# Two layers of cross-attention and expert MLP: last expert of layer 0 finished block by block, two contexts of layer 1 taken ahead, first block of the last stage taken without the block tables

## Chip, cores and metric

The kernel runs on one core of a Trainium2 chip, in one launch. The metric is the device time of that core in microseconds (us), as the median of the runs. All arithmetic shown here is in 32-bit floats. TensorE multiplies, VectorE (DVE), ScalarE (ACT) and GpSimd (POOL) do the rest, and SyncE (SP) issues most of the DMAs.

## What is computed

There are 16 sequences of 128 tokens with 512 features, and one context of 128 rows for each sequence. Four residual steps follow one another:

```python
x = x + L0_xattn(layernorm(x), ctx)      # two attentions, 16 heads
x = x + L0_ffn(layernorm(x))             # 8 experts, top 2, capacity 640
x = x + L1_xattn(layernorm(x), ctx)      # keys/values of context and tokens
x = x + L1_ffn(layernorm(x))             # 8 experts, top 2, no capacity
# L0 expert:  relu(x_e @ w1) @ w2, 512 -> 2048 -> 512, times the gate
# L1_xattn:   k, v from [ctx ; tokens]; q and k RMS-normed, then RoPE
# L1 expert:  (silu(x @ w1_gate) * (x @ w1_up)) @ w2, 512 -> 352 -> 512
```

The change leaves all of this as it is; it concerns the order of the work in the last three steps, and some buffers.

## The kernel before

The program has four stages, one after the other.

**Layer-0 attention** (class `Layer0`) is not touched.

**Layer-0 experts** (`Experts0`). Each of the 8 experts has 640 slots in five blocks of 128 rows. An expert's hidden width of 2048 is cut into 16 slices. `first(e, k)` multiplies the transposed rows of the expert by one slice of w1 in two halves of 320 columns, into the PSUM banks h0 and h1, and applies the relu into `hT` (h0 on ScalarE, h1 on VectorE). `second(e, k)` adds that slice's product with w2 to five PSUM banks o0 to o4, one for each block; each bank has one buffer. The loop in `run` issues `first` one slice ahead of `second`. In the 16th slice `result(e, b)` scales bank b by the gate weight into a tile `y` (even b on ScalarE, odd b on VectorE), and GpSimd adds y into the table in DRAM with an indirect DMA (a scatter). The scatters of one table are chained: each waits for the one before to have landed. The rings are `y` 5 buffers, `hT` 3, `w1` and `w2` 3 each. Gathers of the next expert's rows, the rope tables (`rope_tables`) and the loads of layer 1's weights are spread over the slices as well.

**Layer-1 attention** (`Layer1`). The steps of one sequence are named in the list `ORDER1`, each with a lag in periods; period p takes each step for sequence p minus its lag, so six and more sequences are in flight. Every engine keeps exactly this program order (the class `InOrder` records each instruction in order, which is why its line, L65, stands for nearly all instructions in the profile). For a sequence's context the steps are: `Kp0` (key projection, TensorE), `Ksq0` (squares, ScalarE), `Krs0` (inverse root on GpSimd), `Kn0` (normalise, VectorE), `Ka0` and `Kb0` (the two RoPE products, VectorE and GpSimd), `Ks0` (their sum), `Vp0` and `V0` (value projection and copy), `Ktr0` and `KT0` (transposes and copy). Its tokens go through `ldx` (load), `ln1`, `lnp`, `lnn` (layer norm), `trX` (transpose), `hT` (copy), and then `Vp1`, `Kp1`, `Qp0` and the rest. `load_first` loads the context `cT` and the rope table `rp`. All tiles of this stage lie in the pool `c_work`, which is opened after the experts' pool is closed and takes over its memory. The weights lie in the pool `c_w`, which is opened before the experts' pool.

**Layer-1 experts** (`Blocks1`). The chosen rows are cut into 39 blocks of 128, each of one expert; which, is known only on the chip. At the stage's start SP is given 16 loads of `e_w`, the weights of all 8 experts (1408 KB and 768 KB for each), and after them `rows_behind` (a tile `e_zero` of zeros, written to the spare rows of the output). `tables` then computes from the routing counts which expert and which slots each block has: some twenty small VectorE steps, and at the end two matmuls that pick the slots, and `slot_rows`, which makes of them the rows to gather (`e_source`) and to scatter to (`e_target`). Then a software pipeline runs over the blocks: gather (GpSimd) four periods ahead, transposes, `first` (h0 and h1), `gate` (silu on ScalarE), `product` (VectorE), transposes, `second`, and the scatter into the output. TensorE addresses a block's weights through a register that is loaded from the tables (`register`), and `first` reads from a view that covers the weights of all experts up to the block's largest possible one.

Of the kernel before, what the change touches and what calls it, by code (L numbers as in the profile page):

```python
# [22 lines left out]
P = 128  # L23
# [6 lines left out]
E = 8  # L30
# [842 lines left out]
    )  # L873


def slot_rows(ops, pool, tokens, n):


    nc, t = ops.nc, ops.t
    ids = t(pool, [P, n], F32, "e_ids")  # L880
    nc.vector.tensor_scalar(ids, tokens, -1.0, None, ALU.add)
    source = t(pool, [P, n], I32, "e_source")
    nc.vector.tensor_scalar(source, ids, 0.0, None, ALU.max)
    behind = t(pool, [P, 1], F32, "e_behind")
    nc.vector.tensor_scalar(behind, ops.tok[:, 0:1], float(SPAN + 1), None, ALU.add)
    empty = t(pool, [P, n], F32, "e_empty")
    nc.vector.tensor_scalar(empty, ids, 0.0, behind, ALU.is_lt, ALU.mult)
    target = t(pool, [P, n], I32, "e_target")
    nc.vector.tensor_tensor(target, ids, empty, ALU.add)
    return source, target  # L890

# [54 lines left out]
class Experts0:  # L946
# [4 lines left out]

    SLICES = FF0 // P

    def __init__(self, ops, tc, args, router, x_dram, sum_dram, work, psum):
        self.ops, self.args, self.work, self.psum = ops, args, work, psum
# [20 lines left out]
    def weights(self, e, f):  # L978
        nc, t = self.ops.nc, self.ops.t
        w1 = t(self.work, [P, NC, 256], F32, "w1", 3)  # L980
        nc.sync.dma_start(out=w1, in_=self.args["f0_w1"][e, f])
        w2 = t(self.work, [P, 2, D], F32, "w2", 3)
        nc.sync.dma_start(out=w2, in_=self.args["f0_w2"][e, f])
        self.w[e, f] = w1, w2

    def first(self, e, k):
        nc, t = self.ops.nc, self.ops.t
        if k % 2 == 0:
            self.weights(e, k // 2)
        w1, at = self.w[e, k // 2][0], k % 2 * P  # L990
        hT = self.h[e, k] = t(self.work, [P, CAP], F32, "hT", 3)
        half = CAP // 2
        for i in range(2):
            s = slice(i * half, i * half + half)
            ps = t(self.psum, [P, half], F32, f"h{i}")
            for c in range(NC):
                nc.tensor.matmul(
                    ps, w1[:, c, at : at + P], self.xT[e][:, c, s],
                    start=(c == 0), stop=(c == NC - 1),
                )  # L1000
            if i:
                nc.vector.tensor_scalar(hT[:, s], ps, 0.0, None, ALU.max)
            else:
                nc.scalar.activation(hT[:, s], ps, AF.Relu)

    def second(self, e, k):
        nc, t = self.ops.nc, self.ops.t
        if k == 0:
            self.outs[e] = [t(self.psum, [P, D], F32, f"o{b}") for b in range(NBLK0)]
        hT, w2 = self.h.pop((e, k)), self.w[e, k // 2][1]  # L1010
        for b in range(NBLK0):
            nc.tensor.matmul(
                self.outs[e][b], hT[:, b * P : (b + 1) * P], w2[:, k % 2, :],
                start=(k == 0), stop=(k == self.SLICES - 1),
            )
            if k == self.SLICES - 1:
                self.result(e, b)

    def result(self, e, b):

        nc = self.ops.nc
        y = self.ops.t(self.work, [P, D], F32, "y", 5)
        col = self.column(e, b)
        weight = self.table[:, P + col : P + col + 1]
        if b % 2:
            nc.vector.tensor_scalar(y, self.outs[e][b], weight, None, ALU.mult)
        else:
            nc.scalar.activation(y, self.outs[e][b], AF.Copy, scale=weight)
        scatter_add(self.ops, self.sum_dram, self.target[:, col : col + 1], y)

    def run(self, extra):
        for b in range(NBLK0):
            self.fetch(0, b)
            self.turn(0, b)
        steps = [(e, k) for e in range(E) for k in range(self.SLICES)]
        for i, (e, k) in enumerate(steps):
            self.first(e, k)
            if i:
                self.second(*steps[i - 1])
            if e + 1 < E and k % 2 == 0:  # L1040
                b = k // 2 - 2
                if 0 <= b + 2 < NBLK0:
                    self.fetch(e + 1, b + 2)
                if 0 <= b < NBLK0:
                    self.turn(e + 1, b)
            if i >= 4 and extra:
                extra.pop(0)()
        self.second(*steps[-1])


def layer0_experts(ops, tc, args, router, x_dram, sum_dram, extra):
# [33 lines left out]
class Layer1:  # L1085

    def __init__(self, ops, args, x_rows, w, rope_dram, router, out, work, banks):
        self.ops, self.args, self.x_rows, self.rope_dram = ops, args, x_rows, rope_dram  # L1090
        self.wq, self.wk, self.wv, self.wo = w
        self.router, self.out, self.work, self.banks = router, out, work, banks
        self.at = [{} for _ in range(NB)]

    def load_first(self, b):

        t, nc, s = self.ops.t, self.ops.nc, self.at[b]
        s["cT"] = t(self.work, [P, NC, P], F32, "cT", 2)
        nc.sync.dma_start(out=s["cT"], in_=self.args["ctxT"][b])
        s["rp"] = t(self.work, [P, 3, 2, P], F32, "rp", 3)  # L1100
        nc.sync.dma_start(out=s["rp"].rearrange("p i s h -> p (i s h)"), in_=self.rope_dram[b])

    def load_x(self, b, tag, bufs):
        s = self.at[b]
        s[tag] = self.ops.t(self.work, [P, D], F32, tag, bufs)
        self.ops.nc.sync.dma_start(out=s[tag], in_=self.x_rows[b])

    def step(self, name, b):
# [164 lines left out]
    def run(self):  # L1273
        lags = dict(ORDER1)
        last = max(lags.values())
        for period in range(NB + last):
            for b, call in (
                (period - lags["Kp0"] + 1, self.load_first),
                (period - lags["xr"] + 1, lambda b: self.load_x(b, "xr", 3)),
            ):  # L1280
                if 0 <= b < NB:
                    call(b)
            for name, lag in ORDER1:
                if 0 <= period - lag < NB:
                    self.step(name, period - lag)
            if period >= last:
                self.at[period - last].clear()


def layer1_attention(ops, tc, args, x_rows, w, rope_dram, router, out):  # L1290
    with ExitStack() as ctx:
        work = ctx.enter_context(tc.tile_pool(name="c_work", bufs=1))
        psum2 = ctx.enter_context(tc.tile_pool(name="c_ps", bufs=2, space=PSUM))
# [7 lines left out]
                return pool.tile(shape, dt, name=name, tag=tag)  # L1301

        scheduled, ops.nc = ops.nc, Engines(tc, ops.nc)
        Layer1(ops, args, x_rows, w, rope_dram, router, out, work, Banks()).run()
        ops.nc = scheduled


class Blocks1:
# [8 lines left out]
    def __init__(self, ops, tc, args, router, x_dram, out, small, work, psum):  # L1317
# [1 line left out]
        self.x_dram, self.out, self.work, self.psum = x_dram, out, work, psum  # L1319
        nc, t = ops.nc, ops.t  # L1320
        self.w = t(small, [P, E, FW], F32, "e_w")
        for e in range(E):
            rows = slice(e * P, (e + 1) * P)
            nc.sync.dma_start(out=self.w[:, e, :FW1], in_=args["f1_w1"][rows, :])
            nc.sync.dma_start(out=self.w[:, e, FW1:], in_=args["f1_w2"][rows, :])
        rows_behind(ops, small, out)
        self.tables(small)
        self.at = [{} for _ in range(NBLK1)]

    def tables(self, small):  # L1330

        ops, nc, t, router = self.ops, self.ops.nc, self.ops.t, self.router
        iota = ops.iota
        n = SPAN // P
        pc = t(self.psum, [P, D], F32, "po")
        nc.tensor.matmul(pc[:, :E], ops.ones, router.macc, start=True, stop=True)
        count = t(small, [P, E], F32, "count")
# [42 lines left out]
        nc.vector.scalar_tensor_tensor(place, eb, float(n), place, ALU.mult, ALU.add)  # L1380
        pick = t(small, [P, NBLK1], F32, "pick")
        nc.vector.tensor_scalar(pick, place, ops.tok[:, 0:1], None, ALU.is_equal)
        pi = t(self.psum, [P, D], F32, "po")
        for i in range(2):
            nc.tensor.matmul(
                pi[:, i * P : i * P + NBLK1], router.table[:, i * P : (i + 1) * P], pick,
                start=True, stop=True,
            )
        self.weight = t(small, [P, NBLK1], F32, "e_weight")
        nc.vector.tensor_copy(self.weight, pi[:, P : P + NBLK1])  # L1390
        self.source, self.target = slot_rows(ops, small, pi[:, :NBLK1], NBLK1)

    def gather(self, j, s):
        s["g"] = self.ops.t(self.work, [P, D], F32, "g", 4)
        gather(self.ops, s["g"], self.x_dram, self.source[:, j : j + 1])

    def register(self, j, s):
        last = min(j, E - 1)  # L1400
# [28 lines left out]
    def gate(self, j, s):  # L1429
        s["act"] = self.ops.t(self.work, [P, FF1], F32, "act", 2)  # L1430
        self.ops.nc.scalar.activation(s["act"], s["h", 0], AF.Silu)

    def product(self, j, s):
        self.ops.nc.vector.scalar_tensor_tensor(
            s["act"], s["act"], self.weight[:, j : j + 1], s["h", 1], ALU.mult, ALU.mult
        )

    def turn_act(self, j, s):
# [22 lines left out]
        self.ops.nc.scalar.copy(s["y"], s["po"])  # L1461

    def add(self, j, s):
        scatter_add(self.ops, self.out, self.target[:, j : j + 1], s["y"])

    def run(self):
        self.plain, self.ops.nc = self.ops.nc, Engines(self.tc, self.ops.nc)
# [22 lines left out]
def xattn_moe_two_layers(ctx: ExitStack, tc: tile.TileContext, args, out):  # L1490
# [26 lines left out]
    with tc.tile_pool(name="c_w", bufs=1) as wpool:  # L1517
# [5 lines left out]
        def ahead(work):  # L1523
# [10 lines left out]

        layer0_experts(ops, tc, args, router0, x0_dram, x_dram, ahead)
        layer1_attention(
            ops, tc, args, x_rows, (wq, wk, wv, wo), rope_dram, router1, out
        )
    layer1_experts(ops, tc, args, router1, x1_dram, out)

# [71 lines left out]
```

## Time and profile before

| what | value |
|---|---|
| median of 3 runs | 3967.91 us (3963.16 to 3968.94) |
| profiled execution | 3962.43 us, its span 3960.7 us |
| granted TensorE clock over the span | 0.974 of full |
| layer-0 attention | 0 to about 1390 us |
| layer-0 experts | about 1397 to 2536 us |
| layer-1 attention | about 2568 to 3612 us |
| layer-1 experts | about 3612 to 3960 us |

The profile is of one execution. Its columns of time are microseconds from the span's start. In the timeline, the bracket at the end of a row gives how long the engine was idle before it, and what released it. A matmul of 32-bit floats appears as two instructions, so that a projection with four matmuls of 128x512 is listed as x8. In the names, `o<-w,hT` is an operation that writes tile o and reads w and hT; `x_dram<-y` is a scatter of a y.

### The profile page before, as it was taken

The numbers are of one execution on the slowest core, as the hardware profiler recorded it, in microseconds if no ns is written. First come the engines' busy times: TensorE is split into PE (matmuls) and PEld (weight loads), VectorE is DVE, ScalarE is ACT, GpSimd is POOL, SyncE is SP. The second block draws the span as 40 slices with busy tenths as digits, with TensorE's granted clock in tenths as the row PEclk, the third lists the DMA queues.
The fourth block names the chain that finished last, engine by engine and source line by source line (L and its number), as shares of the span: only waits on it lengthen the run. The fifth ranks groups of instructions, "written<-read, shape, count | busy, mean of one in ns | idle before, by whom it ended". The sixth has DMA issues, their size and how long they took to land. (4 is left out here: it accounts for less than half of the span.)

```text
span 3960.7 us, 44119 instructions
## 1 busy us (share of the span) xinstructions
PE 3762.5 (95%) x14481; PEld 2417.1 (61%) x14481; DVE 1873.6 (47%) x4335; ACT 1369.1 (35%) x5089; POOL 1205.3 (30%) x1488
## 2 busy tenths in 40 slices
PE   5999899899999889999999999699999999997998
PEld 3776677688788755555555555355555555554565
DVE  7878877777788823100000000055555555553111
ACT  4665555566766401000000000043443433341111
POOL 7446655644522123111011000042222222220332
PEclk8999999899999989999999999899999999998999
DMA  5223332322322253233233232200000100005433
GB/s 170 90 94 117 115 105 95 120 91 96 115 81 81 72 191 99 93 90 82 61 91 85 65 85 72 57 22 25 28 31 22 31 22 29 18 11 207 75 65 56
DMA packets 134818, 312.45 MB, mean 79 GB/s; under 512 B 15872, under 2 KB 16000, under 8 KB 132800
## 3 DMA queue, kind: packets, MB, share of 16 engines
q1 hardware_dynamic: 116896, 268.21, 20.8%
q0 software_dynamic: 17696, 41.43, 5.7%
q8 instruction: 117, 1.92, 0.2%
q14 instruction: 109, 0.89, 0.1%
HBM read 231.72 MB, written 77.86 MB: 78 GB/s over the span
## 5 line engine op out<-in xcount | busy, mean ns | idle before, releaser
L65 PE MATMUL h<-xT,w 128*128 128x320 f32 x2048 | 574.8, 434 | 4.1 <-ACT hT L65 4.1
L65 PE MATMUL o<-w,hT 128*128 128x512 f32 x1280 | 570.0, 592 | 0.0
L65 PEld LDWEIGHTS h<-xT,w 128*128 128x128 f32 x2048 | 387.9, 191 | 191.1 <-issue 43.7
L65 DVE TENSOR_SCALAR hT<-h 128x320 f32<-128x320 f32 x128 | 62.9, 492 | 784.4 <-PE h L65 776.3
L65 PEld LDWEIGHTS o<-w,hT 128*128 128x128 f32 x1280 | 243.2, 190 | 265.5 <-issue 245.1
L65 ACT ACTIVATE hT<-h 128x320 f32<-128x320 f32 x128 | 55.8, 436 | 923.0 <-PE h L65 923.0
L65 POOL DMA_INDIRECT x_dram<-y,e_target x40 | 62.8, 1571 | 867.3 <-ACT y L65 717.4
L65 ACT ACTIVATE p<-sc,sm_nm 128x128 f32<-128x128 f32 (+1 forms) x768 | 300.9, 408 | 25.0 <-DVE sm_nm L65 14.4
L65 PE MATMUL mm<-w,xq 128*128 128x512 f32 x1024 | 294.6, 432 | 14.4 <-ACT raw L65 7.6
L65 PE MATMUL po<-w,cq 128*128 128x512 f32 x1024 | 274.2, 410 | 6.3 <-DVE cq L65 6.3
L65 PE MATMUL sc<-kT,qT 128*128 128x128 f32 (+1 forms) x1536 | 266.8, 310 | 5.9 <-ACT p L65 5.9
L65 PEld LDWEIGHTS sc<-kT,qT 128*128 128x128 f32 x1536 | 222.6, 191 | 63.2 <-issue 45.7
L65 PE MATMUL pv<-pT,v 128*128 128x256 f32 (+1 forms) x768 | 257.7, 459 | 1.4 <-ACT pT L65 1.4
L65 ACT ACTIVATE hn_sq<-mm 128x128 f32<-128x128 f32 x768 | 213.3, 278 | 121.1 <-PE mm L65 102.0
L65 DVE TENSOR_REDUCE sm_nm<-sc 128x4 f32<-128x512 f32 (+1 forms) x256 | 176.0, 687 | 140.6 <-PE sc L65 138.9
L65 PEld LDWEIGHTS mm<-w,xq 128*128 128x128 f32 x1024 | 198.8, 200 | 60.0 <-ACT raw L65 8.4
L65 PE MATMUL po<-c_wo,oT 128*128 128x512 f32 x512 | 231.4, 595 | 0.0
L65 PE MATMUL mm<-c_wq,hT 128*128 128x512 f32 x512 | 230.4, 593 | 0.4 <-DVE qn L65 0.4
L65 PEld LDWEIGHTS po<-w,cq 128*128 128x128 f32 x1024 | 185.7, 191 | 42.8 <-DVE cq L65 7.2
L65 POOL TENSOR_TENSOR hn_rs<-hn_rs,mhalf 128x4 f32<-128x4 f32 x192 | 197.2, 1027 | 16.0
L65 ACT ACTIVATE rms_sq<-mm 128x128 f32<-128x128 f32 x384 | 106.8, 278 | 273.2 <-PE mm L65 227.2
L65 PE MATMUL h<-e_w,xT 128*128 (+1 forms) x624 | 199.1, 462 | 1.7 <-DVE xT L65 1.7
(213 smaller groups left out, 6241.8 us busy)
## 6 DMA issues: line engine op xcount, KB each, us to landing
w<-in_f_w SPq DMA_DIRECT2D x128, 512.0 KB, 3.7
x_dram<-xr SPq DMA_DIRECT2D x64, 256.0 KB, 2.0
xr<-x_dram SPq DMA_DIRECT2D x64, 256.0 KB, 2.9
e_w<-in_f_w SPq DMA_DIRECT2D x8, 1408.0 KB, 22.3
xk<-in_ctxT SPq DMA_DIRECT2D x32, 256.0 KB, 2.8
xv<-in_ctxT SPq DMA_DIRECT2D x32, 256.0 KB, 3.3
raw<-in_wproj SPq DMA_DIRECT2D x32, 256.0 KB, 3.0
lnT<-kept_lnT SPq DMA_DIRECT2D x32, 256.0 KB, 3.2
```

What stands on the lines that cost most here:

```text
L65: return self.tc.keep_in_program_order(call(*args, **kwargs))
```

## The change

It has three parts.

- In `Experts0` the last `HELD` = 6 slices of the last expert are not taken slice by slice: their `first` steps run in a row, and then block after block takes all six second products, so that each block's result follows its own six. For this the rings of `hT` and `w2` grow to 7 and 5. The ring of `y` goes from 5 to 3, for all experts.
- In `Layer1` the tiles `cT`, `rp` and `xn` move to the pool `c_w`. The context steps of the first two sequences (`CONTEXT`) are issued ahead of the first period, one sequence after the other, and left out of the periods later.
- In `Blocks1` SP loads only the weights of expert 0 at the start, and `rows_behind` follows at once. The two loads of expert j+1 are issued on ScalarE's queue, behind the silu of block j, for j = 0 to 6. Block 0, which is always the first block of expert 0, gets its slots from the first column of the identity instead of the tables (`slots`), and its gather is issued before the tables are computed; the tables follow, and serve the other blocks (`column`).

```diff
@@ -873,19 +873,19 @@
-def slot_rows(ops, pool, tokens, n):
+def slot_rows(ops, pool, tokens, n, tag="e"):
...
@@ -951,7 +951,9 @@
     SLICES = FF0 // P
+    HELD = 6
     def __init__(self, ops, tc, args, router, x_dram, sum_dram, work, psum):
         self.ops, self.args, self.work, self.psum = ops, args, work, psum
@@ -979,7 +981,7 @@
         nc, t = self.ops.nc, self.ops.t
         w1 = t(self.work, [P, NC, 256], F32, "w1", 3)
         nc.sync.dma_start(out=w1, in_=self.args["f0_w1"][e, f])
-        w2 = t(self.work, [P, 2, D], F32, "w2", 3)
+        w2 = t(self.work, [P, 2, D], F32, "w2", self.HELD // 2 + 2)
         nc.sync.dma_start(out=w2, in_=self.args["f0_w2"][e, f])
         self.w[e, f] = w1, w2
@@ -988,7 +990,7 @@
         if k % 2 == 0:
             self.weights(e, k // 2)
         w1, at = self.w[e, k // 2][0], k % 2 * P
-        hT = self.h[e, k] = t(self.work, [P, CAP], F32, "hT", 3)
+        hT = self.h[e, k] = t(self.work, [P, CAP], F32, "hT", self.HELD + 1)
         half = CAP // 2
         for i in range(2):
             s = slice(i * half, i * half + half)
@@ -1003,12 +1005,12 @@
             else:
                 nc.scalar.activation(hT[:, s], ps, AF.Relu)
-    def second(self, e, k):
+    def second(self, e, k, blocks=range(NBLK0)):
         nc, t = self.ops.nc, self.ops.t
         if k == 0:
             self.outs[e] = [t(self.psum, [P, D], F32, f"o{b}") for b in range(NBLK0)]
-        hT, w2 = self.h.pop((e, k)), self.w[e, k // 2][1]
-        for b in range(NBLK0):
+        hT, w2 = self.h[e, k], self.w[e, k // 2][1]
+        for b in blocks:
             nc.tensor.matmul(
                 self.outs[e][b], hT[:, b * P : (b + 1) * P], w2[:, k % 2, :],
                 start=(k == 0), stop=(k == self.SLICES - 1),
@@ -1019,7 +1021,7 @@
     def result(self, e, b):
         nc = self.ops.nc
-        y = self.ops.t(self.work, [P, D], F32, "y", 5)
+        y = self.ops.t(self.work, [P, D], F32, "y", 3)
         col = self.column(e, b)
         weight = self.table[:, P + col : P + col + 1]
         if b % 2:
@@ -1033,9 +1035,10 @@
             self.fetch(0, b)
             self.turn(0, b)
         steps = [(e, k) for e in range(E) for k in range(self.SLICES)]
+        held = len(steps) - self.HELD
         for i, (e, k) in enumerate(steps):
             self.first(e, k)
-            if i:
+            if 0 < i <= held:
                 self.second(*steps[i - 1])
             if e + 1 < E and k % 2 == 0:
                 b = k // 2 - 2
@@ -1045,7 +1048,9 @@
                     self.turn(e + 1, b)
             if i >= 4 and extra:
                 extra.pop(0)()
-        self.second(*steps[-1])
+        for b in range(NBLK0):
+            for e, k in steps[held:]:
+                self.second(e, k, (b,))
 def layer0_experts(ops, tc, args, router, x_dram, sum_dram, extra):
@@ -1086,8 +1091,14 @@
-    def __init__(self, ops, args, x_rows, w, rope_dram, router, out, work, banks):
+    AHEAD = 2
+    CONTEXT = (
+        "Kp0", "Ksq0", "Krs0", "Kn0", "Ka0", "Kb0", "Ks0", "Vp0", "V0", "Ktr0", "KT0"
+    )
+    def __init__(self, ops, args, x_rows, w, rope_dram, router, out, first, work, banks):
         self.ops, self.args, self.x_rows, self.rope_dram = ops, args, x_rows, rope_dram
+        self.first_pool = first
         self.wq, self.wk, self.wv, self.wo = w
         self.router, self.out, self.work, self.banks = router, out, work, banks
         self.at = [{} for _ in range(NB)]
@@ -1095,14 +1106,15 @@
     def load_first(self, b):
         t, nc, s = self.ops.t, self.ops.nc, self.at[b]
-        s["cT"] = t(self.work, [P, NC, P], F32, "cT", 2)
+        s["cT"] = t(self.first_pool, [P, NC, P], F32, "cT", 2)
         nc.sync.dma_start(out=s["cT"], in_=self.args["ctxT"][b])
-        s["rp"] = t(self.work, [P, 3, 2, P], F32, "rp", 3)
+        s["rp"] = t(self.first_pool, [P, 3, 2, P], F32, "rp", 3)
         nc.sync.dma_start(out=s["rp"].rearrange("p i s h -> p (i s h)"), in_=self.rope_dram[b])
     def load_x(self, b, tag, bufs):
         s = self.at[b]
-        s[tag] = self.ops.t(self.work, [P, D], F32, tag, bufs)
+        pool = self.first_pool if tag == "xn" else self.work
+        s[tag] = self.ops.t(pool, [P, D], F32, tag, bufs)
         self.ops.nc.sync.dma_start(out=s[tag], in_=self.x_rows[b])
     def step(self, name, b):
@@ -1273,21 +1285,29 @@
     def run(self):
         lags = dict(ORDER1)
         last = max(lags.values())
+        self.done = set()
+        for b in range(self.AHEAD):
+            self.load_first(b)
+        for b in range(self.AHEAD):
+            for name in self.CONTEXT:
+                self.step(name, b)
+                self.done.add((name, b))
         for period in range(NB + last):
             for b, call in (
                 (period - lags["Kp0"] + 1, self.load_first),
                 (period - lags["xr"] + 1, lambda b: self.load_x(b, "xr", 3)),
             ):
-                if 0 <= b < NB:
+                if 0 <= b < NB and (call != self.load_first or b >= self.AHEAD):
                     call(b)
             for name, lag in ORDER1:
-                if 0 <= period - lag < NB:
+                if 0 <= period - lag < NB and (name, period - lag) not in self.done:
                     self.step(name, period - lag)
             if period >= last:
                 self.at[period - last].clear()
-def layer1_attention(ops, tc, args, x_rows, w, rope_dram, router, out):
+def layer1_attention(ops, tc, args, x_rows, w, rope_dram, router, out, first):
     with ExitStack() as ctx:
         work = ctx.enter_context(tc.tile_pool(name="c_work", bufs=1))
         psum2 = ctx.enter_context(tc.tile_pool(name="c_ps", bufs=2, space=PSUM))
@@ -1301,7 +1321,7 @@
-        Layer1(ops, args, x_rows, w, rope_dram, router, out, work, Banks()).run()
+        Layer1(ops, args, x_rows, w, rope_dram, router, out, first, work, Banks()).run()
...
@@ -1319,19 +1339,39 @@
         self.x_dram, self.out, self.work, self.psum = x_dram, out, work, psum
         nc, t = ops.nc, ops.t
         self.w = t(small, [P, E, FW], F32, "e_w")
-        for e in range(E):
-            rows = slice(e * P, (e + 1) * P)
-            nc.sync.dma_start(out=self.w[:, e, :FW1], in_=args["f1_w1"][rows, :])
-            nc.sync.dma_start(out=self.w[:, e, FW1:], in_=args["f1_w2"][rows, :])
+        self.load(nc.sync, 0)
         rows_behind(ops, small, out)
+        self.at = [{} for _ in range(NBLK1)]
+        self.blocks = None
         self.tables(small)
-        self.at = [{} for _ in range(NBLK1)]
+    def load(self, queue, e):
+        rows = slice(e * P, (e + 1) * P)
+        queue.dma_start(out=self.w[:, e, :FW1], in_=self.args["f1_w1"][rows, :])
+        queue.dma_start(out=self.w[:, e, FW1:], in_=self.args["f1_w2"][rows, :])
+    def slots(self, small, which, n, tag):
+        nc, table = self.ops.nc, self.router.table
+        ps = self.ops.t(self.psum, [P, D], F32, "po")
+        for i in range(2):
+            nc.tensor.matmul(
+                ps[:, i * P : i * P + n], table[:, i * P : (i + 1) * P], which,
+                start=True, stop=True,
+            )
+        source, target = slot_rows(self.ops, small, ps[:, :n], n, tag)
+        weight = self.ops.t(small, [P, n], F32, f"{tag}_weight")
+        nc.vector.tensor_copy(weight, ps[:, P : P + n])
+        return source, target, weight
     def tables(self, small):
         ops, nc, t, router = self.ops, self.ops.nc, self.ops.t, self.router
         iota = ops.iota
         n = SPAN // P
+        self.block0 = self.slots(small, ops.ident[:, 0:1], 1, "e0")
+        self.gather(0, self.at[0])
         pc = t(self.psum, [P, D], F32, "po")
         nc.tensor.matmul(pc[:, :E], ops.ones, router.macc, start=True, stop=True)
         count = t(small, [P, E], F32, "count")
@@ -1380,21 +1420,18 @@
         nc.vector.scalar_tensor_tensor(place, eb, float(n), place, ALU.mult, ALU.add)
         pick = t(small, [P, NBLK1], F32, "pick")
         nc.vector.tensor_scalar(pick, place, ops.tok[:, 0:1], None, ALU.is_equal)
-        pi = t(self.psum, [P, D], F32, "po")
-        for i in range(2):
-            nc.tensor.matmul(
-                pi[:, i * P : i * P + NBLK1], router.table[:, i * P : (i + 1) * P], pick,
-                start=True, stop=True,
-            )
-        self.weight = t(small, [P, NBLK1], F32, "e_weight")
-        nc.vector.tensor_copy(self.weight, pi[:, P : P + NBLK1])
-        self.source, self.target = slot_rows(ops, small, pi[:, :NBLK1], NBLK1)
+        self.blocks = self.slots(small, pick, NBLK1, "e")
+    def column(self, i, j):
+        return self.blocks[i][:, j : j + 1] if j else self.block0[i]
     def gather(self, j, s):
-        s["g"] = self.ops.t(self.work, [P, D], F32, "g", 4)
-        gather(self.ops, s["g"], self.x_dram, self.source[:, j : j + 1])
+        if "g" not in s:
+            s["g"] = self.ops.t(self.work, [P, D], F32, "g", 4)
+            gather(self.ops, s["g"], self.x_dram, self.column(0, j))
     def register(self, j, s):
         last = min(j, E - 1)
@@ -1429,10 +1466,12 @@
     def gate(self, j, s):
         s["act"] = self.ops.t(self.work, [P, FF1], F32, "act", 2)
         self.ops.nc.scalar.activation(s["act"], s["h", 0], AF.Silu)
+        if j + 1 < E:
+            self.load(self.ops.nc.scalar, j + 1)
     def product(self, j, s):
         self.ops.nc.vector.scalar_tensor_tensor(
-            s["act"], s["act"], self.weight[:, j : j + 1], s["h", 1], ALU.mult, ALU.mult
+            s["act"], s["act"], self.column(2, j), s["h", 1], ALU.mult, ALU.mult
         )
     def turn_act(self, j, s):
@@ -1461,7 +1500,7 @@
         self.ops.nc.scalar.copy(s["y"], s["po"])
     def add(self, j, s):
-        scatter_add(self.ops, self.out, self.target[:, j : j + 1], s["y"])
+        scatter_add(self.ops, self.out, self.column(1, j), s["y"])
     def run(self):
         self.plain, self.ops.nc = self.ops.nc, Engines(self.tc, self.ops.nc)
@@ -1534,7 +1573,7 @@
-            ops, tc, args, x_rows, (wq, wk, wv, wo), rope_dram, router1, out
+            ops, tc, args, x_rows, (wq, wk, wv, wo), rope_dram, router1, out, wpool
...
```

More of the change, by code (lines that the diff above doesn't have):

```diff
@@ L873, in scatter_add @@
     )
-def slot_rows(ops, pool, tokens, n):
+def slot_rows(ops, pool, tokens, n, tag="e"):
     nc, t = ops.nc, ops.t
-    ids = t(pool, [P, n], F32, "e_ids")
+    ids = t(pool, [P, n], F32, f"{tag}_ids")
     nc.vector.tensor_scalar(ids, tokens, -1.0, None, ALU.add)
-    source = t(pool, [P, n], I32, "e_source")
+    source = t(pool, [P, n], I32, f"{tag}_source")
     nc.vector.tensor_scalar(source, ids, 0.0, None, ALU.max)
-    behind = t(pool, [P, 1], F32, "e_behind")
+    behind = t(pool, [P, 1], F32, f"{tag}_behind")
     nc.vector.tensor_scalar(behind, ops.tok[:, 0:1], float(SPAN + 1), None, ALU.add)
-    empty = t(pool, [P, n], F32, "e_empty")
+    empty = t(pool, [P, n], F32, f"{tag}_empty")
     nc.vector.tensor_scalar(empty, ids, 0.0, behind, ALU.is_lt, ALU.mult)
-    target = t(pool, [P, n], I32, "e_target")
+    target = t(pool, [P, n], I32, f"{tag}_target")
     nc.vector.tensor_tensor(target, ids, empty, ALU.add)
```

## Prediction

> **What bounds the kernel now.** I read the page's first part, then the timeline around each of the three places that the change touches, and last the chain of waits there. The page gives the frame:
>
> ```profile
> span 3960.7 us, 44119 instructions
> ...
> PE 3762.5 (95%) x14481; PEld 2417.1 (61%) x14481; DVE 1873.6 (47%) x4335; ACT 1369.1 (35%) x5089; POOL 1205.3 (30%) x1488
> ```
>
> TensorE works for 3762.5 of 3960.7 us. A gain must come from its 198 us of gaps, and a new wait of TensorE costs its full length wherever the stage has no gap. The layer-0 expert stage (about 1397 to 2536) has none but one of 4.11 us, so what happens at its expert boundaries matters. Timeline at one of the seven, columns start, length, engine, operation, in brackets the idle time before:
>
> ```profile
> 2398.67 4.45 PE L65 MATMUL o<-w,hT 128*128 128x512 f32 x10
> 2400.70 1.62 POOL L65 DMA_INDIRECT x_dram<-y,e_target  x1 [101.29 <-ACT y L65]
> 2406.20 1.58 POOL L65 DMA_INDIRECT x_dram<-y,e_target  x1 [3.88 <-DMA x_dram<-y,e_target]
> 2407.27 4.45 PE L65 MATMUL o<-w,hT 128*128 128x512 f32 x10
> 2413.84 1.56 POOL L65 DMA_INDIRECT x_dram<-y,e_target  x1 [6.07 <-issue]
> ```
>
> The five results leave PSUM within 5 us, but their scatters follow one another 5.5 to 7.6 us apart (row 2 to 5), while TensorE writes the same five banks again from 2407.27 (row 4). Today five `y` buffers keep the two apart.
>
> Layer 0 to layer 1, the chain of waits and then the timeline:
>
> ```profile
> 2557.02 4.91 DMA x_dram<-y,e_target
> ```
> ```profile
> 2567.64 5.97 PE L65 MATMUL mm<-c_wk,cT 128*128 128x512 f32 x8 [31.24 <-DMA cT<-in_ctxT]
> 2573.45 0.60 PE L65 MATMUL tr<-ident,xn 128*128 128x128 f32 x4
> ```
>
> The last matmul of layer 0 ends at X = 2536.39; the fifth scatter ends at 2561.93, and only then do SP's loads start. TensorE idles 31.24 us and starts cold (5.97 us for 8 matmuls that take 3.43 later). The tokens' first transpose comes at X+37.06.
>
> Layer-1 attention to its experts, the chain and the timeline:
>
> ```profile
> 3611.70 5.93 DMA e_w<-in_f_w
> 3617.65 25.65 DMA e_w<-in_f_w
> 3643.37 18.33 DMA out_x<-e_zero
> ```
> ```profile
> 3620.89 1.08 POOL L65 DMA_INDIRECT g<-x_dram,e_source  x1 [8.59 <-DVE e_empty L887]
> 3628.66 1.11 PE L65 MATMUL tr<-ident,g 128*128 128x128 f32 x4 [8.62 <-DMA g<-x_dram,e_source]
> 3630.56 6.60 PE L65 MATMUL h<-e_w,xT 128*128 128x352 f32 x16 [0.78 <-DVE xT L65]
> 3638.52 2.63 PE L65 MATMUL h<-e_w,xT 128*128 x8 [0.92 <-DVE xT L65]
> ```
>
> Gather 0 waits for the block tables and then takes 7.7 us among sixteen weight loads. From block 1 (3638.52) TensorE is the bound, 8.08 us a block.
>
> **Part by part.** *Three `y` buffers instead of five.* The last expert needs no more, but the count holds for all eight. With T the start of an expert's last o group (2398.67 above), y3 takes y0's buffer, free at the end of scatter 0 (about T+6.8), and is done before its bank is wanted (second(e+1,0) block 3, T+8.6+3x0.86 = T+11.2). y4 takes y1's buffer, free when scatter 1 has landed, which is 0.69 us before scatter 2 is issued. So y4 (0.69 us on ScalarE) ends about when scatter 2 is issued, plus 0.1; TensorE wants its bank at T+8.6+4x0.86 = T+12.04. Scatter 2 is issued at T+15.08, 15.19, 15.56, 14.76, 14.68, 16.26, 15.16 at the seven boundaries, so TensorE stands for 3.25, 3.62, 2.82, 2.74, 4.32, 3.22 at the last six (the boundary shown is the last): 20.0 us. Behind the waiting y4 on ScalarE stands the next slice's relu (0.44 us); TensorE asks for it one group later, so it adds nothing. The first boundary's stall I cost at nothing: the 4.11 us gap at 1584 to 1588 (rope tables on POOL) comes a few us later and covers it; uncovered it is 3.1.
>
> Does the clock fall in these stalls? The rows: after 3.22 us of idle (3601.02) a transpose took 0.63, full speed; after 4.11 us (1588.35) 16 matmuls took 6.26 instead of 4.47, that is 1.8 more. The Trainium skill, "TensorE: Matmul & The Clock Gate", Part 1, puts the limit at one idle window of about 3.4 us. By the rows only the 4.32 us stall surely pays (+1.8, sum 21.8); by the rule the 3.62 us one does too (+3.6, sum 23.6). I take 22. From both sides: scatter 1 took 7 us above where the others take 5.5, beside weight loads that the two more w2 buffers now let go earlier; without that each y4 comes 1.5 us sooner, sum 11. High end 24.
>
> *Block by block at the end of the last expert.* The same 320 o matmuls and h matmuls in another order; TensorE's work is the same, and the relus keep their 0.44 to 0.49 us beside 4.3 us of matmuls a slice, so the order itself costs nothing, nor do the larger hT and w2 rings; were a relu late, it would show as a gap, a few tenths. Result b comes 12x0.43 = 5.16 us apart, as the scatters do (5.5), so scatter 4 ends at about X+0.9+5.5+1 = X+7.5 instead of X+25.5.
>
> *Two contexts ahead.* cT and rp leave the pool that takes the experts' memory, so SP loads them early. Kp0(0) may start at about X+1. The squares write a tile of the new pool, whose memory the experts hold until the last scatter has read y, and all of that is tied to X+7.5: squares at X+8.2. From the rows per context: squares 1.6, POOL rsqrt 1.3, normalise 0.7, the two POOL products 1.92, sum 0.7, waits 0.4, so 6.6, then the transpose 0.5. Ktr0(0) ends at X+15.3; Kp0(1) follows it cold, 5.97 instead of 3.43, to X+21.3; 6.6 more gives X+27.9. The tokens' ln1 on DVE, rsqrt on POOL and lnn (0.69+0.18+0.15+0.55+0.55 and hand-overs, 2.3) stand behind these in each queue: first token transpose at X+30 against X+37.06, a gain of 7. Then hT no longer stands behind the squares (before, 2575.24 instead of 2574.0), 1 more. And later periods lose Kp0(1), Vp0(0), Vp0(1), 3x3.43, and two transposes, 2x0.5: 11.3 us of TensorE, which between 2570 and 2600 is busy 27.45 of 30 us and later fully. I credit 70 %, 8. Sum -16. Ends: if the squares don't wait for the pool, the chain is 7 us earlier, -24; if the freed work leaves only gaps, -8. The first tokens' load stands on SP behind nothing long: cT, rp are issued before.
>
> *Last stage.* Two small matmuls (1.05 us for the like on the 3618.99 row) and six DVE operations of about 0.2 go ahead of the tables: gather 0 is issued at about 3613.8 instead of 3620.89 and lands by 3619, while the tables end 1.3 later, 3622.1. The copy xT(0) stands behind the tables on DVE, so h(0) starts at about 3622.9, not 3630.56: -7.7. Its first half ends cold at +4.3, 3627.2. ScalarE's gate(0) waits for that, and the load of expert 1 stands behind gate(0) on that queue. It moves 1408+768 KB at the 415 GB/s of this stage, 5.4, plus 2.0 of a small load (page, 256 KB): it lands at 3634.7, so block 1 starts 3.7 earlier than 3638.52 instead of 7.7, and the new 4 us gap makes it cold, +1.8. e_zero is issued at once, and the 0.8 us stall at 3668 that it caused goes: together -3.
>
> Issuing them takes ScalarE's queue 14 times 0.33 to 0.45 us (SP's rows today), on an engine that is busy for a sixth of this stage (49 of 300 us): nothing.
>
> For loads 2 to 7 the trace of before shows no DMA on ScalarE's queue. The Trainium skill, "Perfetto Trace Analysis", DVE / Act Engine Instruction, has the sequencer free for the next instruction as soon as one is pushed into the wait queue. Then loads 2 and 3 go out while gates 1 and 2 still wait, every load is periods ahead, and the part is worth -3. Without it each load is issued when its gate runs: the second rival. No row decides; near it stands only that TensorE reads each block's weight register between queued matmuls without a gap. I take the run-ahead, and keep +18 as the other end.
>
> Sum: +22 -16 -3 = +3 on the profiled execution of 3962.4 (span 3960.7 and 1.7 around it), 3965. The median of the runs, 3967.9, lies 5.5 above it, so 3971.
>
> **Rivals.** *Slower: loads paced by the gates.* If ScalarE's queue issues load j+1 only when gate(j) has started, a period is the load (7.4) plus h's first half (2.37 on the later chain), the hand-overs (0.3), and up to 2.9 us of the block's own gather and scatter on the same engines, say 11.7 instead of 8.08. That decides as soon as it exceeds 8.08. Six periods cost 21.7; less 3.7 of the start, +18: +22 -16 +18 = +24, 3992. For it: in-order issue, and no load there today. Against: the rule above.
>
> *Faster: the y wait is mild and the context chain free.* Scatters of 5.5 us (+11), squares at X+1 (-24), -3: -16, 3952. For it: scatters here do take 5.5 where no weights move. Against: all seven boundaries show the longer wait.
>
> *It does not do what it says:* the context steps fill only time in which the tokens' chain would wait anyway, and the first period ends nearly where it did: +22 -4 -3 = +15, 3983.
>
> **How the numbers follow.** Forecast 0.45 (own range 3960 to 3980), slower rival 0.28, faster 0.15, no gain 0.12. A measurement can tell 0.2 %, 8 us, from no change: faster is below 3960, slower above 3976. Faster: most of the fast rival and a little of the forecast, 0.18. Slower: the slow rival, most of the no-gain case and a quarter of the forecast, 0.44. Same 0.38. Range 3952 to 3998.
>
> **What would show it.** Right: at each layer-0 boundary y4 on ScalarE just ahead of scatter 2, and an o matmul with some 3 us of idle before it, released by it; first context matmul within 3 us of the last o, squares after the last scatter, first token transpose near X+30; loads of experts 2 and 3 issued beside load 1, block period 8.1. Wrong: scatter 1 landing before T+11.5 (no stall); squares at X+1; ScalarE issuing one load per period with TensorE waiting for `e_w`.

## The result, and the profile after

The changed kernel takes 4001.81 us (median of 4 runs, 3992.75 to 4004.55) beside 3968.43 us for the kernel before in the same session: 1.0083 of it (95 % interval 1.0065 to 1.0101). It is slower by some 33 us, where I had forecast 3971, within the 8 us that count as no change, with a range to 3998; of the three outcomes I had given "slower" the largest chance, 0.44. The profiled execution has a span of 4002.8 us against 3960.7.

Cut at the same instructions, the two profiled spans differ by 42.1 us, which is more than the medians do: the profiled execution of the changed kernel is the slowest of its four, and that of before lies 5.5 us below its median. X is the end of layer 0's last matmul, R the end of the last update of the routing table (row `r_table`). The change does not touch the first row; its 3.4 us belong to no part of it.

| stretch | before | after | difference | my sum |
|---|---|---|---|---|
| up to the first transpose of the layer-0 experts | 1403.3 | 1406.7 | +3.4 | 0 |
| layer-0 experts, to X | 1133.1 | 1160.0 | +26.8 | +22 |
| layer-1 attention, X to R | 1075.6 | 1067.6 | -8.1 | -16 |
| layer-1 experts, R to the end | 348.7 | 368.6 | +19.9 | -3 |

The page of the changed kernel: its first part, two of the groups (their last column is the idle time of the engine ahead of them, and what ended most of it), and the row of ScalarE's loads (KB each, and the median us from issue to landing):

```profile
span 4002.8 us, 44121 instructions
PE 3791.7 (95%) x14485; PEld 2430.3 (61%) x14485; DVE 1874.8 (47%) x4341; ACT 1368.7 (34%) x5089; POOL 1206.6 (30%) x1488
...
L65 PE MATMUL o<-w,hT 128*128 128x512 f32 x1280 | 575.8, 596 | 20.1 <-ACT y L65 20.1
...
L65 PE MATMUL h<-e_w,xT 128*128 (+1 forms) x624 | 209.1, 480 | 18.9 <-DMA e_w<-in_f_w 12.3
...
e_w<-in_f_w ACTq DMA_DIRECT2D x7, 1408.0 KB, 7.8
```

The same two groups on the page of before:

```profile
L65 PE MATMUL o<-w,hT 128*128 128x512 f32 x1280 | 570.0, 592 | 0.0
L65 PE MATMUL h<-e_w,xT 128*128 (+1 forms) x624 | 199.1, 462 | 1.7 <-DVE xT L65 1.7
```

Two waits are new: 20.1 us ahead of o matmuls, ended by a y, and 18.9 us ahead of the last stage's first matmuls, 12.3 of it ended by a weight load. TensorE is also busy 29 us longer with nearly the same instructions, which points to its clock.

The same expert boundary as in the prediction, timeline of the changed kernel:

```profile
2431.89 1.58 POOL L65 DMA_INDIRECT x_dram<-y,e_target  x1 [3.99 <-DMA x_dram<-y,e_target]
2438.45 0.69 ACT L65 ACTIVATE y<-o,r_table 128x512 f32<-128x512 f32 x1 [10.73 <-DMA x_dram<-y,e_target]
2439.07 1.56 POOL L65 DMA_INDIRECT x_dram<-y,e_target  x1 [5.60 <-DMA x_dram<-y,e_target]
...
2439.18 1.90 PE L65 MATMUL o<-w,hT 128*128 128x512 f32 x2 [2.73 <-ACT y L65]
2440.88 5.43 PE L65 MATMUL h<-xT,w 128*128 128x320 f32 x16
```

The fifth y waits for scatter 1 to land (row 2), TensorE waits 2.73 us for that y (row 4), and then runs at half speed: two o instructions in 1.90 us instead of 1.02 at full clock, sixteen h instructions in 5.43 instead of 4.47.

The start of layer 1's attention, timeline:

```profile
2567.45 3.70 PE L65 MATMUL mm<-c_wk,cT 128*128 128x512 f32 x8 [0.78 <-ACT y L65]
2575.41 0.28 ACT L65 ACTIVATE rms_sq<-mm 128x128 f32<-128x128 f32 x1 [8.01 <-DMA x_dram<-y,e_target]
2581.96 1.11 PE L65 MATMUL tr<-ident,ra 128*128 128x128 f32 x4 [7.37 <-DVE ra L65]
2594.59 0.66 PE L65 MATMUL tr<-ident,ra 128*128 128x128 f32 x4 [3.05 <-DVE ra L65]
2596.91 1.09 PE L65 MATMUL tr<-ident,xn 128*128 128x128 f32 x4 [1.65 <-DVE xn L65]
```

The 31 us gap is gone, the first context projection runs 0.8 us after X = 2566.67, the squares come at X+8.7 behind the last scatter, and the tokens' first transpose at X+30.2. And the last stage, where ACTq is ScalarE's queue issuing a load:

```profile
3649.08 0.86 ACTq L65 DMA_DIRECT2D e_w<-in_f_w  x2
3657.00 4.76 PE L65 MATMUL h<-e_w,xT 128*128 x8 [5.33 <-DMA e_w<-in_f_w]
3661.60 0.49 PE L65 MATMUL tr<-ident,act 128*128 128x128 f32 x3
...
3662.13 0.37 ACT L65 COPY aT<-tr 128x256 f32<-128x256 f32 x1 [11.35 <-PE tr L65]
3662.14 0.34 ACTq L65 DMA_DIRECT2D e_w<-in_f_w  x1
3662.40 0.47 ACT L65 ACTIVATE act<-h 128x352 f32<-128x352 f32 x1
...
3668.25 2.60 PE L65 MATMUL h<-e_w,xT 128*128 x8 [0.77 <-DMA e_w<-in_f_w]
...
3727.24 5.03 PE L65 MATMUL h<-e_w,xT 128*128 x8 [2.89 <-issue]
```

The load of expert 2 goes out at 3662.14, one block after expert 1's (3649.08) and not beside it. It passes the gate that stands ahead of it (3662.40), but not the copy aT before that, which had to wait for the transposes (3662.13). The load's own record has no semaphore to wait for, so it was the queue that held it. This closes a ring: the transposes come behind the first half of block 1's h (3661.60 behind 3657.00), and that h waits for the load of expert 1. So no load can go out before the one ahead of it has landed and the first half of h has used it.

### The profile page after: what moved, and what is told of

It reads as the page before. It is cut to its first block, busy times and chain, and to the rows that moved or that the text cites. A ratio compares the mean times of both kernels' runs of the same rounds, so it can differ in the third digit from the quotient of the medians.

```text
span 4002.8 us, 44121 instructions
## 1 busy us (share of the span) xinstructions
PE 3791.7 (95%) x14485; PEld 2430.3 (61%) x14485; DVE 1874.8 (47%) x4341; ACT 1368.7 (34%) x5089; POOL 1206.6 (30%) x1488
## 3 DMA queue, kind: packets, MB, share of 16 engines
q1 hardware_dynamic: 114880, 252.61, 20.1%
## 4 chain that ended last, share of the span: by engine, by line
PE 85%; DVE 5%; DMA 4%; issue 2%; POOL 2%; ACT 1%; SPq 0%; POOLq 0%; ACTq 0%; DVEq 0%
PE mm L65 25%; PE h L65 18%; PE po L65 12%; PE o L65 12%; PE tr L65 7%; PE pv L65 5%; PE sc L65 5%; DMA x_dram<-y,e_target 2%; DMA e_w<-in_f_w 1%; DVE q_m L65 1%; DVE mean L65 1%; DVE cut L65 1%; POOL w L65 0%; DVE p L65 0%; ACT hn_sq L65 0%
## 5 line engine op out<-in xcount | busy, mean ns | idle before, releaser
L65 PE MATMUL o<-w,hT 128*128 128x512 f32 x1280 | 575.8, 596 | 20.1 <-ACT y L65 20.1
L65 PE MATMUL h<-e_w,xT 128*128 (+1 forms) x624 | 209.1, 480 | 18.9 <-DMA e_w<-in_f_w 12.3
L65 POOL TENSOR_SCALAR hn_rs<-hn_ss,ws 128x4 f32<-128x4 f32 x160 | 67.5, 422 | 437.5 <-ACT hn_sq L65 437.3
```

The lines of the kernel that those rows point to most:

```text
L65: return self.tc.keep_in_program_order(call(*args, **kwargs))
```

## The experiments

Theory: the time was lost to two rings of waits, the y buffers and the paced loads, and the context chain gave back most of what the blockwise end, with the pool of cT, rp and xn, won. The rivals stand in the expectations. All ratios are to the kernel before, run beside them on the same chip.

**1. Five y buffers again.**

```diff
-        w2 = t(self.work, [P, 2, D], F32, "w2", self.HELD // 2 + 2)
+        w2 = t(self.work, [P, 2, D], F32, "w2", self.HELD // 2 + 1)
...
-        y = self.ops.t(self.work, [P, D], F32, "y", 3)
+        y = self.ops.t(self.work, [P, D], F32, "y", 5)
```

> The changed kernel with five y buffers again (to make room, the w2 ring is 4 instead of 5; everything else as changed). Theory A (y4 waits for scatter 1 to hand back its buffer, TensorE stands 2.9 us for its bank, and the clock then falls): all seven stalls go; the stage of layer-0 experts loses 26.8 us against the changed kernel (20.1 of stalls, about 12 of half clock, less the 5.9 of the gap near 1584 that comes back), so about 3975. Theory B (the stalls come from the bigger rings' loads colliding with the scatters, or from the new order): they stay, about 4002.

Measured: 3971.65 us, 1.0016 (1.0009 to 1.0022). The experts take 1136.0 us, all seven stalls are gone, and the 4.13 us gap at 1590 (before: 4.11) is back:

```profile
L65 PE MATMUL o<-w,hT 128*128 128x512 f32 x1280 | 569.4, 592 | 0.0
```

Theory A holds. In the stage that this edit doesn't touch, layer-1 experts, this run took 355.5 us and not 368.6. Timeline of this kernel, first halves of h of blocks 1 and 7:

```profile
3632.50 2.60 PE L65 MATMUL h<-e_w,xT 128*128 x8 [2.94 <-DMA e_w<-in_f_w]
...
3693.34 2.60 PE L65 MATMUL h<-e_w,xT 128*128 x8 [2.56 <-issue]
```

The loads pace these blocks as well, but with a period of (3693.34-3632.50)/6 = 10.14 us instead of the 11.71 of the changed kernel's profile. The last section shows the clock's part in this.

**2. Three y buffers in the kernel before.**

```diff
-        y = self.ops.t(self.work, [P, D], F32, "y", 5)
+        y = self.ops.t(self.work, [P, D], F32, "y", 3)
```

> The kernel before with three y buffers instead of five, nothing else. Theory A: seven stalls of 2.7 to 3.5 us at the expert boundaries, some with half clock after them: 25 to 30 us slower than before, about 3996. Theory B: as before, 3968.

Measured: 3991.71 us, 1.0071 (1.0058 to 1.0085); the experts take 1156.8 us, 23.7 more than before. The page line of this kernel:

```profile
L65 PE MATMUL o<-w,hT 128*128 128x512 f32 x1280 | 575.7, 596 | 20.2 <-ACT y L65 20.2
```

The ring of y alone makes the stalls, without the new order or the larger rings.

**3. All weights of the last stage on SP.**

```diff
         rows_behind(ops, small, out)
+        for e in range(1, E):
+            self.load(nc.sync, e)
...
-        if j + 1 < E:
-            self.load(self.ops.nc.scalar, j + 1)
```

> The changed kernel with all expert weights of the last stage on SP at its start, behind expert 0's and the zeros; ScalarE's queue issues none. Theory C (each load waited on ScalarE's queue behind the instruction that waits for the block before, so seven blocks were paced by a load): the last stage goes from 369 us to 342 to 345, about 3976. Theory D (the loads themselves, or contention with gathers and scatters, are the limit and not where they are issued): 360 us or more for the stage, 3993 or more.

Measured: 3971.58 us, 1.0017 (1.001 to 1.0024); the last stage takes 341.0 us, 27.6 less than in the changed kernel and 7.7 less than before. Theory C holds. TensorE waits for no load:

```profile
L65 PE MATMUL h<-e_w,xT 128*128 (+1 forms) x624 | 200.5, 465 | 1.7 <-DVE xT L65 1.7
```

**4. No context ahead.**

```diff
-    AHEAD = 2
+    AHEAD = 0
```

> The changed kernel with no context taken ahead (AHEAD = 0); the blockwise end and the pool of cT, rp and xn stay. Theory E (the two contexts' chain, run in order on every engine, holds up the tokens: the first token transpose at X+30 where the loads alone would allow X+19, X being the end of layer 0's last matmul): the transpose comes at X+17 to X+20, and layer-1 attention is as long as in the changed kernel or up to 8 us shorter, 3994 to 4002. Theory F (the work taken ahead is worth its 11 us): it is 4 to 11 us longer, 4006 to 4013.

Measured: 3980.84 us, 1.0047 (1.0033 to 1.006). Theory E holds, and by more than it said: the first token transpose comes at X+13.6, and the attention takes 1054.3 us, 13.3 less than with two contexts ahead. Timeline of this kernel, X = 2565.50:

```profile
2566.28 3.70 PE L65 MATMUL mm<-c_wk,cT 128*128 128x512 f32 x8 [0.78 <-ACT y L65]
2576.56 0.69 DVE L65 BATCH_NORM_STATS2 ln_st<-xn 128x6 f32<-128x512 f32 x1 [15.36 <-DMA xn<-x_dram]
2579.08 1.12 PE L65 MATMUL tr<-ident,xn 128*128 128x128 f32 x4 [9.11 <-DVE xn L65]
```

The layer norm starts as soon as its load is there, at X+11; in the changed kernel the tokens were as early in memory, but VectorE took them at X+27.8, behind both contexts.

**5. The loads one block earlier, on the same queue.**

```diff
         self.load(nc.sync, 0)
+        self.load(nc.sync, 1)
...
-        if j + 1 < E:
-            self.load(self.ops.nc.scalar, j + 1)
+        if j + 2 < E:
+            self.load(self.ops.nc.scalar, j + 2)
```

> The changed kernel with the loads of the last stage one block earlier: expert 1's go out on SP after expert 0's, and ScalarE's queue issues those of expert j+2 behind gate(j). Same queue, same waits, one period (8 us) more of lead against a load of about 7.8 us. Theory C (the lead is what is missing: a load on ScalarE's queue goes out when the instruction before it has what it waits for): TensorE's waits for the weights nearly go, last stage 341 to 346 us, about 3973. Theory G (issuing on ScalarE's queue is itself slow, or delays the activations): waits of 1 to 3 us a block stay, 353 us or more, 3983 or more.

Measured: 3973.27 us, 1.002 (1.001 to 1.003); the last stage takes 342.0 us, and TensorE waits for no load:

```profile
L65 PE MATMUL h<-e_w,xT 128*128 (+1 forms) x624 | 199.9, 464 | 1.7 <-DVE xT L65 1.7
```

Theory C again: the loads are still issued on ScalarE's queue, and one block of lead was what they missed.

**6. Both repairs.** Edits 1 and 3 together.

> The changed kernel with both repairs: five y buffers (w2 ring 4) and all expert weights on SP at the start of the last stage; two contexts stay ahead. If the parts add up, by the stages of the single runs: experts 1136, layer-1 attention 1067, last stage 341 us, 9 us faster than before, about 3956 (ratio 0.998). If one repair uncovers a wait that the other hid, 3965 or more.

Measured: 3948.51 us, 0.9958 (0.9945 to 0.9972), some 8 us better than expected; about 4 of them because the three stages that it names are 13 us below before, not 9. Experts 1135.2, attention 1067.3, last stage 341.8: the stages add up. The ratios of 1 and 3, multiplied and divided by the changed kernel's, give 0.9950.

**7. Both repairs, no context ahead.** Edits 1, 3 and 4.

> As the last, with no context taken ahead. Theory E: layer-1 attention 1054 us, first token transpose near X+14, in all 22 us faster than before, about 3943 (ratio 0.9943). Theory F: not faster than the last run, 3956 or more.

Measured: 3933.08 us, 0.9921 (0.9907 to 0.9935). Attention 1053.8, as in run 4; the total is 10 us better than expected, mostly because it was built on 9 us for run 6, which came out as 18. What is left of the change is the blockwise end, the pool of cT, rp and xn, and block 0 taken without the tables.

**8. Only the first context's projections ahead.** On run 7:

```diff
-    AHEAD = 0
+    AHEAD = 1
-    CONTEXT = (
-        "Kp0", "Ksq0", "Krs0", "Kn0", "Ka0", "Kb0", "Ks0", "Vp0", "V0", "Ktr0", "KT0"
-    )
+    CONTEXT = ("Kp0", "Vp0", "V0")
```

> As the last, but the first context's key and value projections and the copy of the value (Kp0, Vp0, V0 of sequence 0) are issued ahead, nothing else. They fit in the gap ahead of the first token transpose (9.1 us with no context ahead), so if only the vector chain was what hurt, the attention is 3 us shorter than with nothing ahead, about 3940; if even the copy on ScalarE (0.6 us, waiting for the last scatter) holds up what follows, it is the same or up to 2 us longer.

Measured: 3930.78 us, 0.9913 (0.99 to 0.9927). The gap ahead of the token transpose shrinks from 9.15 to 5.62 us and the transpose stays at X+13.5, but the attention is only 1.3 us shorter, 1052.5. The interval overlaps that of run 7, so the step is not resolved. It has the lowest median here.

**9. One context ahead.** On run 7, AHEAD = 1 with the whole list.

> Both repairs, and one context taken ahead whole (AHEAD = 1) instead of two or none. Theory E (the tokens wait behind the contexts' chain on DVE and GpSimd): with one chain of 6.6 us behind the last scatter the first token transpose comes at X+17 to X+19, between X+13.6 (none) and X+30.1 (two); layer-1 attention 1053 to 1059 us. If the loss came with the second context's cold projections alone, the transpose comes at X+14 and the attention takes 1050 to 1053.

Measured: 3937.23 us, 0.9928 (0.9911 to 0.9945); transpose at X+17.7, attention 1057.3. Both as theory E had them.

**10. Two contexts ahead, step by step in turn.** On run 6:

```diff
-        for b in range(self.AHEAD):
-            for name in self.CONTEXT:
+        for name in self.CONTEXT:
+            for b in range(self.AHEAD):
```

> Both repairs, two contexts ahead, but their steps taken in turn (Kp0 of 0, Kp0 of 1, Ksq0 of 0, ...) instead of one sequence after the other. Theory E, and in it the part of the serial order: the two chains overlap, only GpSimd's share (3.2 us a context) is added, so the first token transpose comes at X+19 to X+22 and the attention takes 1056 to 1061 instead of 1067 us. If the amount of work ahead is what costs, and not its order: X+28 to X+30, 1065 to 1068.

Measured: 3940.58 us, 0.9937 (0.992 to 0.9953). The attention takes 1059.4 us, as expected, but the transpose comes at X+24.2, later than expected. Timeline:

```profile
2540.09 7.13 PE L65 MATMUL mm<-c_wk,cT 128*128 128x512 f32 x16 [0.78 <-ACT y L65]
2552.22 10.09 PE L65 MATMUL mm<-c_wv,cT 128*128 128x512 f32 x16 [5.00 <-DVE qn L65]
2559.39 0.55 DVE L65 TENSOR_SCALAR xn<-xn,ln_mv,ln_rs 128x512 f32<-128x512 f32 x1 [0.67 <-POOL ln_rs L65]
2563.47 0.66 PE L65 MATMUL tr<-ident,xn 128*128 128x128 f32 x4 [0.29 <-ACT kT L65]
```

The two key projections (row 1) hold both PSUM buffers of their ring, so the value projections (row 2) wait until `Kn0` of the first sequence has read its own, and after this idle time they run partly at half clock. The tokens' layer norm is done at 2559.94 (row 3), but their transpose stands behind these projections on TensorE (row 4). So the serial order costs at least 8 of the 13 us (1067.3 to 1059.4). The other 5.6 are what work ahead costs in this order, this new wait included; what it costs by itself was not separated.

## Why the prediction was wrong

**The loads on ScalarE's queue: the step that failed.** I took the statement of the Trainium skill ("Perfetto Trace Analysis", DVE / Act Engine Instruction) that the sequencer is free once an instruction is pushed into the wait queue, and let loads 2 and 3 go out beside load 1. They didn't. In this trace a load on ScalarE's queue passes an instruction that is only waiting for its turn, not one whose wait is unmet (3662.13, 3662.14, 3662.40 above). I put -3 for the stage and 19.9 came: 22.9 of the 39 us by which the sum of the parts was too low. The other 16 are 7.9 in the attention, 4.8 in layer 0's experts and the 3.4 of the first row. The rival that I gave 0.28 had the mechanism nearly right (the copy ahead of the gate holds the load, not the gate itself), and its price fits: a period of 11.7 us, which the rows show as (3727.24-3657.00)/6 = 11.71, and +18 for the stage. That the fit is so close is luck. Three of the six periods hold a first half of h at half clock (4.76 or 5.03 us instead of 2.60), which the rival did not count. Without its allowance for gathers and scatters its period is 10.07, near the 10.14 in the profile of run 1, where the clock stayed full in these blocks and the stage was only 6.8 us longer than before. That profile is the mild end: by the medians, moving the loads to SP gained 23 us from run 1 to run 6, and 26 from the changed kernel to run 3. With the rival the sum would have been 3992. Runs 3 and 5 show the cause: the loads issued on SP, or one block earlier on the same queue, end the waits. The first steps of the stage were right: h(0) starts at R+10.6 (I had 3622.9, R+10.9). One reading was wrong: the 2.0 us that I took for a small load is the page's row of a store (x_dram<-xr), while its loads of 256 KB take 2.8 to 3.3. It matters little, since the loads here took 7.8 us by the median against my 7.4.

**The y ring: right wait, wrong clock.** Seven stalls of 2.73 to 3.04 us, 20.1 in all, against 20.0 for six. This was the term that was too small: I charged the clock with one drop of 1.8, and the profile has 23.9 us of half clock in this stretch, in 5 places, which at half speed is about 11.9. And I left the gap near 1584 standing to cover the first stall; instead it went, with its own slow matmuls, 4.11+1.8 = 5.9. So 20.1+11.9-5.9 = 26.1, and measured is 26.8.

**Two contexts ahead: the chain right, its worth wrong.** Squares at X+8.7 (I had 8.2), transpose at X+30.2 (X+30): the -7 is there, as 6.8. Of the 8+1 that I credited for work taken out of later periods 1.3 is left. This credit is the term that failed here. In its place the trace shows TensorE waiting, in the window that was to be full: 1.81 us at 2622.28 and 3.15 at 2627.43, the second for the next tokens' layer norm, and half clock from 2596.4 to 2603.2 and from 2627.1 to 2630.5. A larger error is in how I valued this part. I set the transpose against X+37 of the kernel before, but without any context ahead it already comes at X+13.6 (run 4): the blockwise end and the pool of cT, rp and xn, which no run takes apart, bring 1075.6-1054.3 = 21.3 us, and the contexts ahead give 13.3 back. I had the tokens rightly behind the chain on VectorE and GpSimd, but I did not ask how early they would be without it.

**The rivals.** "Faster" fell: the y waits were full, and the squares do wait for the last scatter. Whether they would start earlier with their tile outside the experts' memory was not tried. "It does not do what it says" was right in that the work taken out of later periods earned nearly nothing (1.3 of 9 us); against run 4 it was not merely no gain but a loss of 13.3.

## What to carry to other kernels

A ring is sized by the stage that turns it fastest: the last expert produced a y every 5 us and had no stall with three, the seven before it produced five in 5 us and stalled every time. A load issued behind a compute instruction inherits that instruction's waits, so count the lead from the last wait that it stands behind, and give it at least the load's time. Before work is moved ahead of a critical chain, price it against what that chain could do without it, queue by queue, and not against the kernel before.

## What the runs showed of the hardware

The clock's drop isn't set by the length of a stall. In the clock record every change of the granted clock lies on a grid of 3.413 us. In the 35 stalls of 2.5 to 3.2 us in five kernels that have a ring of three y (the changed one and runs 2 to 5), half clock followed in the next grid window exactly when enough of one window was idle: 19 stalls with 2.06 us or more in one window all led to it, 16 with 2.01 or less in any window all didn't, though their whole lengths overlap (2.64 to 3.18 and 2.55 to 3.08). The windows view of the changed kernel around three stalls, of 2.88, 2.82 and 2.89 us, each cut at the grid (columns: length; busy time of PE, PEld, DVE, ACT, POOL; granted clock; DMA share; GB/s):

```profile
1568.99:1572.40 3.41, 0.62 (x2) 0.00 (x0) 0.00 (x0) 0.64 (x2) 0.02 (x1) 1.00 0.62 153
1572.41:1575.82 3.41, 3.33 (x5) 1.80 (x6) 2.75 (x13) 1.06 (x5) 1.54 (x1) 0.50 0.41 43
1712.36:1715.77 3.41, 1.81 (x5) 0.50 (x3) 0.00 (x0) 0.00 (x0) 0.00 (x0) 1.00 0.84 192
1715.77:1719.18 3.41, 2.19 (x7) 1.40 (x8) 0.00 (x0) 1.01 (x2) 1.56 (x1) 1.00 0.23 10
1855.72:1859.13 3.41, 1.30 (x4) 0.23 (x2) 0.00 (x0) 0.00 (x0) 0.00 (x0) 1.00 0.74 196
1859.13:1862.54 3.41, 2.62 (x4) 1.40 (x5) 0.00 (x0) 1.01 (x2) 1.55 (x1) 0.50 0.27 16
```

TensorE busy 0.62 or 1.30 of 3.41 us is followed by 0.50, busy 1.81 by 1.00. The Trainium skill ("TensorE: Matmul & The Clock Gate", Part 1) speaks of an idle window of about 3.4 us; here the window's length agrees, but it need not be idle throughout. The limit holds beyond these stalls, but it is not sharp. Counted over all windows at full clock in the twelve profiles, from the first clock record on, the 266 with 2.06 us or more of idle time were all followed by half clock, of the 12,773 with less than 1.8 us one was, and of the 92 between them 64 were. The 3.22 us of idle that I had read as harmless was cut in two by the grid (1.89 and 1.33). With the 0.73 us of idle behind it the second window had 2.06, and half clock did follow, from 3603.1 on, 2 us behind the row that I had read. The grid also bears on the paced stage, which took 368.6 us in one profile and 355.5 in run 1: with waits of 0.4 to 5.3 us ahead of the blocks the first had 27 us of half clock (four times 6.83) from block 1 on, the second, with waits of 0.8 to 2.9 us, none.
